# The loads of the attention weights move from SP's queue to GpSimd's

## The chip, the cores and the metric

The kernel runs on one core of one Trainium2 chip. The metric is the device time of one execution in microseconds (us). Before the change the median of 3 runs is 724.13 us (721.79 to 724.44). A core has these engines: PE (TensorE, matmuls; its weight loads are shown as PEld), DVE (VectorE), ACT (ScalarE), POOL (GpSimd) and SP (SyncE), and 16 DMA engines that move data between DRAM and the on-chip memory. Each engine runs its own instructions in order and waits on semaphores for the others.

## The reference, cut to what matters

The reference is one transformer layer: cross attention of 8 batches of 112 tokens (width 512) to 375 context rows (width 256) with 16 heads of 128, and then a feed-forward part whose weights and activations are rounded to whole numbers of 8 bits. All of it is float32 outside the rounding.

```python
q = rmsnorm((layernorm(x) @ Wq).reshape(B, Sq, H, D), gq)       # Wq: 512 x 2048
k = rmsnorm((ctx @ Wk).reshape(B, Skv, H, D), gk)               # Wk: 256 x 2048
v = (ctx @ Wv).reshape(B, Skv, H, D)                            # Wv: 256 x 2048
attn = softmax(einsum('bqhd,bkhd->bhqk', q, k) / sqrt(D))
x = x + einsum('bhqk,bkhd->bqhd', attn, v).reshape(B, Sq, H * D) @ Wo   # Wo: 2048 x 512
x = x + ffn(layernorm(x))          # two matmuls, rows and weights rounded, gelu between
```

## The kernel before, in words

The attention runs over 4 pairs of batches and, in each pair, over 4 groups of 4 heads: 16 *groups* (G), each of which has two *units* (u = 2G and 2G + 1), one for each batch of the pair. The weights of a group are one slice each: wq (1024 KB), wk (512 KB), wv (512 KB) and wo (1024 KB). They don't stay on the chip between the pairs, so each group loads its own four: 16 loads each of wq, wv and wo, and 15 of wk by the same function, as the first slice of wk comes in two halves (`load_half`, L222).

In a unit, PE makes the keys (`keys`, L632, tile pkk) out of the context and wk. ACT copies them out of PSUM and squares them, DVE sums, scales and transposes them in blocks of 32 (tile kz). The whole transposition goes by DRAM: `key_send` (L689) writes kz to kd with four DMAs, `key_fetch` (L696) reads it back as kT. The queries (`queries`, L514, tile pq, of wq) go by qz, qd (L569) and qr (L601) in the same manner, and ACT makes qT of qr (L608). PE makes the scores out of kT and qT (`scores`, L740, tile sc), DVE and ACT the probabilities, and these go by pz, pd (`prob_send`, L789) and pT (`prob_fetch`, L799). PE weighs the context with pT (`weigh`, L842, tile pu), and both units of a group together go through wv (`values`, L869, tile po) and wo (`project`, L889, tile pw; for the last group `project_rows`, L912). The tokens (xd, xr, xnT) and the context rows (cd, cr) have their own ways by DRAM. The feed-forward part of the batches that are done (ph L1079, py L1158) is woven in between; its weights are loaded in pieces at the start (`load_piece`, L307), and `max_weight` finds their largest magnitude with an all-reduce over partitions on GpSimd (L322), twice in all.

What runs when is written out by hand: four scripts of words (L1214 to L1364, played by `play`), in which `lq`, `lk`, `lv`, `lo` are the four loads and a number after the dot is the group. `in_written_order` (L77) then chains the instructions of PE, DVE, ACT and SP so that each keeps the order of the script:

```python
ORDERED = (ENG.PE, ENG.DVE, ENG.Activation, ENG.SP)
```

GpSimd isn't in this list (L26). On it, the framework's scheduler decides the order, from the instructions' dependencies.

All loads and all transfers by DRAM are issued by SP, in the script's order. So a weight load goes out when SP comes to it and its buffer is free. The buffers: wk has two, wq, wv and wo one each. The load of group 1's wq takes wo's buffer, that of the last wo takes wq's, and that of the last wv takes one of wk's. A load waits until the last matmul that reads the tenant before is done. The framework also gives each DMA that SP issues one of eight completion semaphores in turn, and many an issue waits until the DMA that had this semaphore before has landed.

Of the kernel before, what the change touches and what calls it, by code (L numbers as in the profile page):

```python
# [30 lines left out]
def xattn_ffn_kernel(  # L31
# [16 lines left out]
    nc = tc.nc  # L48
    P = 128
# [7 lines left out]
    NG = INNER // (HG * D)  # L57
    GW = HG * D
# [65 lines left out]
    n = 1  # L124
# [84 lines left out]

    def load_wq(G):  # L210
        t = wpool.tile([P, KC, GW], F32, tag="wo" if G == 1 else "wq", name=f"wq_{G}")
        nc.sync.dma_start(out=t, in_=wq[:, bass.ts(G % NG, GW)].rearrange("(k p) n -> p k n", p=P))
        T["wq", G] = t

    def load_wk(G):
        t = T["wk", G] = wpool.tile([P, KCC, GW], F32, tag="wk", name=f"wk_{G}", bufs=2)
        if G > 0:
            nc.sync.dma_start(out=t, in_=wk[:, bass.ts(G % NG, GW)].rearrange("(k p) n -> p k n", p=P))

    def load_half(k):  # L220

# [3 lines left out]
    def load_wv(G):  # L225
        tag, bufs = ("wk", 2) if G == NGG - 1 else ("wv", 1)
        t = wpool.tile([P, KCC, GW], F32, tag=tag, name=f"wv_{G}", bufs=bufs)
        nc.sync.dma_start(out=t, in_=wv[:, bass.ts(G % NG, GW)].rearrange("(k p) n -> p k n", p=P))
        T["wv", G] = t

    def load_wo(G):
        t = wpool.tile([P, HG, C], F32, tag="wq" if G == NGG - 1 else "wo", name=f"wo_{G}")
        nc.sync.dma_start(out=t, in_=wo[bass.ts(G % NG, GW), :].rearrange("(h p) c -> p h c", p=P))
        T["wo", G] = t

    def pad_context(b):
# [26 lines left out]
    def load_biases(_):  # L263
        after(("jr", 2 * NP - 1))
        nc.sync.dma_start(out=b1_sb, in_=b1.partition_broadcast(P))
        nc.sync.dma_start(out=b2_sb, in_=b2.partition_broadcast(P))

    step("lq", NG, load_wq)
    step("lk", NG, load_wk)
    step("lv", NG, load_wv)  # L270
    step("lo", NG, load_wo)
    step("cz", BP, pad_context)
    step("lc", BP, load_context)
# [1127 lines left out]
```

## Time and profile before

| | us |
|---|---|
| median of 3 runs | 724.13 |
| lowest, highest | 721.79, 724.44 |
| the profiled execution | 723.51 |
| its span, from the first instruction to the last | 721.4 |
| granted TensorE clock in it (mean) | 0.999 |

In the profile's rows, a line such as "pq<-wq,xnT" tells the tile that is written and those that are read, "L514" the line of the kernel, and a row of waits has the total, the number and the longest. The DMA part gives for each transfer the number of issues, the size and the median time from issue to landing:

| transfer | issues | KB each | median us to landing |
|---|---|---|---|
| kd<-kz (keys out) | 128 | 192 | 4.8 |
| kT<-kd (keys back) | 32 | 768 | 5.8 |
| pT<-pd (probabilities back) | 31 | 672 | 6.0 |
| qr<-qd (queries back) | 26 | 224 | 5.7 |
| wq<-in_wq | 16 | 1024 | 8.1 |
| wo<-in_wo | 16 | 1024 | 7.9 |
| wv<-in_wv | 16 | 512 | 5.9 |
| wk<-in_wk | 15 | 512 | 6.0 |

These 63 loads of the four weights are 15 x 0.5 + 16 x 0.5 + 32 x 1 = 47.5 MiB, or 49.8 of the 191.85 MB that the one queue moves. A DMA's "landing" is the time at which its last completion count arrives.

### The profile page before, as it was taken

The page shows a single profiled execution, that of the slowest core. Times are in us where ns is not written, and L with a number is a line of the kernel's source. Part 1 is how long each engine was busy: PE and PEld are TensorE (multiplying, and loading weights), DVE is VectorE, ACT ScalarE, POOL GpSimd, SP SyncE. Part 2 cuts the span into 40 slices and gives each one's busy share as a digit, 9 for nine tenths or more (in the row PEclk, how much of TensorE's full clock was granted, in tenths as well). Part 3 has the DMA queues.
Part 4 walks back from the last instruction along what each step waited for, and adds up shares of the span by engine and source line. Part 5 has one row for each costly group of instructions (what it writes and reads, how often), then busy time and mean ns, then how long its engine had stood idle before and what let it go on. Part 6 is the DMA issues. An engine that isn't in the chain of part 4 may idle for free.

```text
span 721.4 us, 8447 instructions
## 1 busy us (share of the span) xinstructions
PE 701.9 (97%) x2324; PEld 404.1 (56%) x2324; DVE 541.6 (75%) x1249; ACT 437.7 (61%) x1128; POOL 2.7 (0%) x10
## 2 busy tenths in 40 slices
PE   7999999999999999999999999999999999999986
PEld 3444474746557474655556566555665546576642
DVE  6897988768778798668655878687864788874686
ACT  3677757646485764666727564784755477545555
POOL 0000000000000000000000000000000000000000
PEclk9999999999999999999999999999999999999999
DMA  8899999989998999998999889999899998997300
GB/s 265 266 332 313 283 310 357 270 284 331 316 319 279 296 275 277 304 267 273 294 294 294 281 244 285 290 258 296 252 226 308 295 250 263 246 273 267 89 15 29
DMA packets 134125, 192.36 MB, mean 267 GB/s; under 512 B 35184, under 2 KB 93168, under 8 KB 133440
## 3 DMA queue, kind: packets, MB, share of 16 engines
q1 hardware_dynamic: 134080, 191.85, 86.6%
q8 instruction: 18, 0.29, 0.2%
q14 instruction: 27, 0.22, 0.1%
HBM read 126.81 MB, written 61.71 MB: 261 GB/s over the span
## 4 chain that ended last, share of the span: by engine, by line
PE 70%; DMA 17%; DVE 5%; ACT 4%; SPq 2%; issue 1%; DVEq 0%; ACTq 0%
PE pkk L632 17%; PE pu L842 15%; PE pq L514 10%; PE pw L889 9%; PE sc L740 8%; PE po L869 6%; DMA qr<-qd 3%; PE ph L1079 2%; DMA pT<-pd 2%; DMA wq<-in_wq 2%; DMA cT<-in_ctxT 2%; DMA kT<-kd 2%; DMA kd<-kz 1%; DMA wo<-in_wo 1%; DMA qss<-s 1%
## 5 line engine op out<-in xcount | busy, mean ns | idle before, releaser
L632 PE MATMUL pkk<-wk,cT 128*128 128x512 f32 x372 | 170.2, 592 | 0.1
L842 PE MATMUL pu<-pT,c 128*128 128x448 f32 (+1 forms) x384 | 152.0, 540 | 1.9 <-DMA pT<-pd 1.6
L762 ACT ACTIVATE probs<-sc,bias,rq 112x375 f32<-112x375 f32 x128 | 84.4, 664 | 50.5 <-DVE bias L755 48.6
L842 PEld LDWEIGHTS pu<-pT,c 128*128 128x128 f32 (+1 forms) x384 | 72.3, 190 | 74.1 <-issue 62.2
L632 PEld LDWEIGHTS pkk<-wk,cT 128*128 128x128 f32 x372 | 70.2, 190 | 73.9 <-issue 63.6
L514 PE MATMUL pq<-wq,xnT 128*128 128x512 f32 x224 | 101.1, 594 | 3.9 <-DMA wq<-in_wq 2.7
L889 PEld LDWEIGHTS pw<-oT,wo 128*128 128x128 f32 x480 | 90.8, 190 | 8.4 <-issue 4.4
L740 PE MATMUL sc<-kT,qT 128*112 128x384 f32 x256 | 93.9, 487 | 1.4 <-DMA kT<-kd 0.9
L889 PE MATMUL pw<-oT,wo 128*128 128x224 f32 x480 | 94.6, 352 | 0.0
L652 ACT COPY kk<-pkk 128x512 f32<-128x512 f32 x96 | 55.4, 580 | 61.9 <-PE pkk L632 25.0
L663 DVE TENSOR_REDUCE kss<-ksq 128x4 f32<-128x512 f32 x96 | 63.4, 669 | 32.9 <-ACT ksq L657 32.2
L779 DVE STREAM_TRANSPOSE pz<-probs 128x384 f32<-128x384 f32 x124 | 66.1, 556 | 14.8 <-ACT probs L773 13.6
L773 ACT ACTIVATE probs<-probs,inv 112x375 f32<-112x375 f32 x128 | 72.6, 600 | 5.5 <-DVE inv L770 3.8
L753 DVE TENSOR_REDUCE top<-sc 112x1 f32<-112x375 f32 x128 | 63.8, 536 | 15.8 <-PE sc L740 15.5
L514 PEld LDWEIGHTS pq<-wq,xnT 128*128 128x128 f32 x224 | 42.1, 190 | 55.8 <-issue 48.0
L680 DVE STREAM_TRANSPOSE kz<-kk 128x512 f32<-128x512 f32 x96 | 64.9, 693 | 8.6 <-DMA kd<-kz 6.8
L740 PEld LDWEIGHTS sc<-kT,qT 128*112 128x112 f32 x256 | 44.7, 177 | 42.6 <-issue 19.0
L657 ACT ACTIVATE ksq<-kk 128x512 f32<-128x512 f32 x96 | 59.6, 628 | 8.0 <-DVE kss L663 7.5
L670 DVE TENSOR_TENSOR kk<-kk,rk 128x512 f32<-128x512 f32 x96 | 62.9, 676 | 0.3
L853 ACT COPY wc<-pu 128x448 f32<-128x448 f32 x64 | 33.2, 528 | 38.0 <-PE pu L842 38.0
L869 PEld LDWEIGHTS po<-wc,wv 128*128 128x128 f32 x272 | 49.1, 190 | 7.4 <-issue 3.1
L869 PE MATMUL po<-wc,wv 128*128 128x224 f32 (+1 forms) x272 | 52.9, 344 | 0.0
(122 smaller groups left out, 597.7 us busy)
## 6 DMA issues: line engine op xcount, KB each, us to landing
kd<-kz SPq DMA_DIRECT2D x128, 192.0 KB, 4.8
kT<-kd SPq DMA_DIRECT2D x32, 768.0 KB, 5.8
pT<-pd SPq DMA_DIRECT2D x31, 672.0 KB, 6.0
pd<-pz SPq DMA_DIRECT2D x93, 192.0 KB, 3.8
wq<-in_wq SPq DMA_DIRECT2D x16, 1024.0 KB, 8.1
wo<-in_wo SPq DMA_DIRECT2D x16, 1024.0 KB, 7.9
wv<-in_wv SPq DMA_DIRECT2D x16, 512.0 KB, 5.9
wk<-in_wk SPq DMA_DIRECT2D x15, 512.0 KB, 6.0
```

The costliest lines, as they stand in the source:

```text
L514: nc.tensor.matmul(pq[:, :GW], T["xnT", p][:, k, i * P : (i + 1) * P], T["wq", G][:, k, :], start=(k == 0), stop=(k == KC - 1),)
L632: nc.tensor.matmul(pk[:, :GW], T["cT", batch_of(u)][:, k, j * P : (j + 1) * P], T["wk", u // BP][:, k, :], start=(k == 0), stop=(k == KCC ...
L663: nc.vector.tensor_reduce(T["kss", u][:, j, :], T.pop(("ksq", u, j)).rearrange("p (h d) -> p h d", d=D), AX.X, ALU.add)
L680: nc.vector.transpose(T["kz", u][:, :, j, :, :].rearrange("p a h r -> p h a r"), T["kk", u][:, j, :].rearrange("p (h a r) -> p h a r", h=H ...
L740: nc.tensor.matmul(sc[:S, :SKP].rearrange("p (j i r) -> p j i r", j=NJ, r=BK), T["qT", G, i][:, h, :], T["kT", u][:, :, :, h, :].rearrange ...
L753: nc.vector.tensor_reduce(top[:, h : h + 1], T["sc", u, h0 + h][:S, :SK], AX.X, ALU.max, negate=True)
L762: nc.scalar.activation(p_bufs[h][:S, :SK], T["sc", u, h][:S, :SK], AF.Exp, bias=T["bias", u, h0][:, h - h0 : h - h0 + 1], scale=rq_of(u, h ...
L773: nc.scalar.mul(p_bufs[h][:S, :SK], p_bufs[h][:S, :SK], T["inv", u][:, h : h + 1])
L779: nc.vector.transpose(T["pz", u][:, :, :, :, h, :].rearrange("p a f j q -> p j a f q"), p_bufs[h].rearrange("p (j a r) -> p j a r", j=NJ, ...
L842: nc.tensor.matmul(pu[:, : HG * S], T["c", b][: ROWS[j], j, k * P : (k + 1) * P], T["pT", u][: ROWS[j], :, j, :, :].rearrange("p f h q -> ...
L869: nc.tensor.matmul(po[:, (h - h0) * n : (h - h0 + 1) * n], T["wv", G][:, k, h * D : (h + 1) * D], T["wc", G][:, k, h, :, :].rearrange("p b ...
L889: nc.tensor.matmul(pw[:, (c - c0) * n : (c - c0 + 1) * n], T["wo", G][:, h, c * P : (c + 1) * P], T["oT", G][:, h, lo : lo + n], start=(h ...
```

## The change

The four functions that load a group's weights issue their DMA on GpSimd (`nc.gpsimd`) instead of SP (`nc.sync`). Source, destination, size and the place of the call in the script are the same. `load_half`, the loads of x, context, gains, biases and feed-forward weights, and all transfers by DRAM stay on SP.

```diff
     def load_wq(G):
         t = wpool.tile([P, KC, GW], F32, tag="wo" if G == 1 else "wq", name=f"wq_{G}")
-        nc.sync.dma_start(out=t, in_=wq[:, bass.ts(G % NG, GW)].rearrange("(k p) n -> p k n", p=P))
+        nc.gpsimd.dma_start(out=t, in_=wq[:, bass.ts(G % NG, GW)].rearrange("(k p) n -> p k n", p=P))
         T["wq", G] = t
...
         if G > 0:
-            nc.sync.dma_start(out=t, in_=wk[:, bass.ts(G % NG, GW)].rearrange("(k p) n -> p k n", p=P))
+            nc.gpsimd.dma_start(out=t, in_=wk[:, bass.ts(G % NG, GW)].rearrange("(k p) n -> p k n", p=P))
...
-        nc.sync.dma_start(out=t, in_=wv[:, bass.ts(G % NG, GW)].rearrange("(k p) n -> p k n", p=P))
+        nc.gpsimd.dma_start(out=t, in_=wv[:, bass.ts(G % NG, GW)].rearrange("(k p) n -> p k n", p=P))
...
-        nc.sync.dma_start(out=t, in_=wo[bass.ts(G % NG, GW), :].rearrange("(h p) c -> p h c", p=P))
+        nc.gpsimd.dma_start(out=t, in_=wo[bass.ts(G % NG, GW), :].rearrange("(h p) c -> p h c", p=P))
```

## The prediction, made before the changed kernel was run

> **What bounds the kernel now.** I read the shares of the engines first, then the DMA queues, the stretches, the waits of PE and of SP, and last the timeline around single loads. The first part of the page and the row of its 40 slices for DMA:
>
> ```profile
> PE 701.9 (97%) x2324; PEld 404.1 (56%) x2324; DVE 541.6 (75%) x1249; ACT 437.7 (61%) x1128; POOL 2.7 (0%) x10
> DMA  8899999989998999998999889999899998997300
> q1 hardware_dynamic: 134080, 191.85, 86.6%
> ```
>
> PE is idle for 721.4 - 701.9 = 19.5 us, GpSimd nearly always. All bytes go by one queue. The stretches (us, then busy time of PE, PEld, DVE, ACT, POOL, granted clock, DMA share, GB/s) tell where PE's idle time is:
>
> ```profile
> 0.00:20.00 20.00, 16.33 (x32) 7.12 (x33) 12.11 (x50) 7.48 (x18) 1.67 (x8) 1.00 0.82 261
> 20.00:100.00 80.00, 80.00 (x225) 40.24 (x224) 70.36 (x160) 58.02 (x177) 0.71 (x1) 1.00 0.93 300
> 100.00:200.00 100.00, 98.12 (x311) 57.83 (x310) 80.25 (x171) 59.83 (x158) 0.00 (x0) 1.00 0.94 314
> 300.00:400.00 100.00, 97.22 (x323) 57.97 (x322) 64.86 (x144) 58.11 (x151) 0.00 (x0) 1.00 0.94 284
> 660.00:721.00 61.00, 52.75 (x258) 30.75 (x257) 40.53 (x92) 32.54 (x55) 0.00 (x0) 0.99 0.23 66
> ```
>
> 3.7 us lie before 20, 8.3 after 660, where no weight is loaded; only 7.5 us lie between. DMA is at 0.93 to 0.94 of its time there: the second resource that is nearly full, whose order of work can cost PE time. PE's waits that a DMA ended, and three of SP's on a weight:
>
> ```profile
> PE pq L514 <- DMA wq<-in_wq: 2.7, 2, 1.4
> ...
> PE pu L842 <- DMA pT<-pd: 1.6, 3, 1.1
> ...
> PE pq L514 <- DMA xnT<-xld: 1.2, 2, 0.7
> PE sc L740 <- DMA kT<-kd: 0.9, 2, 0.6
> ```
>
> ```profile
> SPq L689 <- DMA wq<-in_wq: 5.4, 3, 2.8
> SPq L689 <- DMA wo<-in_wo: 4.6, 2, 2.5
> SPq L569 <- DMA wq<-in_wq: 3.4, 2, 2.5
> ```
>
> So weights delay PE by 2.7 us in all, and they hold up SP's sends of keys (L689) and queries (L569). SP's waits that end at a weight's landing add up to 31.0 us over all eleven such groups, but most are hidden: the whole of PE's DMA waits in these four rows is 6.4 us.
>
> **The change, part by part.** PE, DVE and ACT keep their instructions and order. SP loses 63 DMAs (15 wk, 16 each of wq, wv, wo); GpSimd gains them. The order on GpSimd isn't that of the script: the built program has it by the time at which each load's buffer comes free. I set each load's free time (end of the last matmul on the buffer's tenant before) against its need (first matmul on the new one) from the matmuls' times in the trace. Before, SP issues most loads 10 to 45 us after their buffer is free (wq of group 4: free 98.1, issued 138.9, needed 151.0). On GpSimd nothing holds them. The two maxima (L322), which stand in the same queue, ran at 96.1 and 204.1; the loads behind them come free at 98.1 and 218.6, so they cost nothing; were the first as late as 131, the wo load of group 1 (needed 135.0) would be late.
>
> (a) *Lateness.* The smallest rooms from free to need are wq 6: 13.2 us, wo 14: 13.6, wq 9: 13.9, wo 13: 16.0, wo 10: 17.9, wq 3: 18.2. A wq took 5.0 / 8.1 / 12.8 us (min, median, max) from issue to landing, a wo 6.4 / 7.9 / 11.7. Even at the maximum they land in time. PE's two waits on wq (at 190.0 and 358.1) go, as these loads leave 21.7 and 4.7 us earlier: -2.7.
>
> (b) *The start.* Four loads (wk 1, wq 0, wv 0, wq 1: 512 + 1024 + 512 + 1024 KB) have no predecessor in their buffers. GpSimd's memsets end at 2.2, so all 3 MB can be queued some 3 us into the span; before, they left at 5.7, 6.5, 21.1 and 30.3. They meet the loads that PE waits for:
>
> ```profile
> 1.65 4.82 DMA cT<-in_ctxT
> 6.47 0.14 issue
> 6.60 8.42 PE pkk L642 x12
> ```
>
> This stretch of the chain is start, length, what. x landed at 3.40; the next wk and cT halves, 443.5 KB, took the 3.07 us until 6.47. Sharing the engines half and half from there would double that: +3.1 at most, 0 if GpSimd's first bytes come after 6.5. The rest has a little spare (the x pair lands at 9.7 and DVE waits 2.75 us for it, then has 1.9 us idle at 12.5). I take +2.0, nearer the upper end because GpSimd is free so early.
>
> (c) *Issue time and SP's waits.* A load's issue took SP about 0.43 us, 63 x 0.43 = 27 us in all, and the 31.0 us above go too. On the path this is worth between 0 and the 3.7 us that PE waits for pT, xnT and kT. I take -1.2, a third: most of these fetches wait for their own stores (SP's rows on kd and pd are 14.7 and 14.2 us).
>
> The Trainium skill, "DMA: Bandwidth & Descriptors", section on issuing engines not being separate DMA queues, says that all issuers share the same 16 DMA engines and that a second issuer only saves issue time. Going by it alone, (c) would be the whole gain and (a) no more than a matter of order; the rows on PE's wq waits say that order is worth 2.7.
>
> (d) *Collisions.* Loads that leave 20 us earlier run beside other transfers than before. For every fetch with under 2 us from landing to first use I compared the time that loads are in flight from its store to its landing, before and with the new issue times (a landing as before, stretched to half rate). Most meet less, but these, with next to no spare, meet more: qr landing at 110.6 (4.8 to 14.3 us), kT at 277.3 (8.9 to 13.2), kT at 325.3 (0 to 9.8: wo 6 and wk 10 now leave at 312.1 and 313.8), pT at 328.5 (0 to 4.4).
>
> ```profile
> 321.16 0.34 SPq L696 DMA_DIRECT2D kT<-kd  x1
> 323.32 0.34 SPq L799 DMA_DIRECT2D pT<-pd  x1
> ...
> 325.48 2.81 PE L740 MATMUL sc<-kT,qT 128*112 128x384 f32 x8 [0.26 <-DMA kT<-kd]
> ```
>
> That kT landed 4.1 us after its issue with no weight beside it; the median is 5.8 and the maximum 9.3. So a collision costs 5.8 - 4.1 = 1.7, at most 5.2. Three at 1.7 less 0.1 of spare, and 0.8 for pT (5.2 there against a median of 6.0): 1.6 x 3 + 0.8 = 5.6; bounds 0 and 4 x 5.2 = 20.8. PE then stops in order, and score, exponential and sends behind it move along. I take +5.0, since a stall gives spare to the next.
>
> (e) *Making the transfers on GpSimd.* No row has a DMA issued by GpSimd. Its time to issue is bounded below by SP's 0.43 us and above, as an estimate, by the 5.0 us that remain of the smallest room after a median landing (13.2 - 8.1): past this, loads come late. Beside it, DVE could be held up. DVE's 2048-wide TENSOR_SCALAR takes 1287 ns where the 2048-wide TENSOR_REDUCE takes 2272: it runs nearly twice as fast for an element, on some 55 us of such work in all. If each of 63 loads held DVE for as long as GpSimd's all-reduce took (mean 532 ns), that were 33 us of DVE time, a quarter of it (DVE's idle share is 25%) perhaps on the path: 0 to +8. I take +1.0, because only 8% of the span is such work.
>
> The skill speaks against the change here: "SBUF — State Buffer", section "SBUF: two separate sides", says that a GpSimd-issued DMA has its descriptors written by GpSimd's cores, which a two-port VectorE operation locks out until it ends. By it the 1287 ns above are the longest delay of a load, under every room in (a), so the sum by it has 0 for (e).
>
> **Sum.** -2.7 + 2.0 - 1.2 + 5.0 + 1.0 = +4.1 us. The profiled execution took 723.51 us with its span of 721.4; 723.51 + 4.1 = 727.6. The median of the runs shown, 724.13, is 0.6 above that execution, so I forecast 728.2, 0.6% over it.
>
> **Rivals.** *Weights out of SP's way* (faster): small transfers no longer queue behind 1 MB, so every wait of PE on a DMA goes and nothing is lost at the start or to collisions: 724.13 - 6.4 = 717.7. For it: most tight fetches meet less load, and SP's 31.0 us. Against: DMA stays at 0.94 full. It decides if the median landing of kT falls below about 4.8 us, one under today's.
>
> *Nothing moves* (same): the start's loss takes up the gain at the waits (+2.0 - 2.7 + 0.5 of (c) and (d) together), 724. For it: PE's idle time between 20 and 660 is but 7.5 us, and most loads have over 20 us of room. Against: tight fetches at 0.0 to 0.1 us.
>
> *Late loads* (much slower): if a 1 MB load takes 20 us from GpSimd's issue, the six rooms above are short by 6.8, 6.4, 6.1, 4.0, 2.1 and 1.8: +27, some 751; at 16 us it is +7.3 by the first three (2.8, 2.4, 2.1), which on top of the forecast without the gain of (a) is 728.2 + 2.7 + 7.3 = 738. For it: no row prices a GpSimd DMA. Against: rooms half as large again as the median landing.
>
> That the change doesn't do what it says: the order isn't the same, as shown; that is within the sum.
>
> **How the numbers follow.** Chances: the forecast 0.38 (its own range 727.8 to 735), late loads 0.12, same 0.25, weights out of the way 0.25. Runs of this kernel differ by about 0.4% (721.79 to 724.44), so 0.5% is about what a measurement tells from none: slower 0.50, same 0.25, faster 0.25. The range for 8 in 10 leaves out a little of the faster case below 717 and most of the late loads above 738; it holds (b) and (c) at both ends and (d) up to half its upper bound.
>
> **What would show it.** A second queue in the DMA part with 49.8 MB. (a) No row PE L514 <- DMA wq; loads issued at their buffers' free times. (b) The first pkk L642 later than 6.60, by 0 to 3.1. (c) SP's waits on w loads gone. (d) More of PE's waits on kT, pT and of ACT on qr, at about 110, 277 and 320 to 330; kT's median landing above 5.8. (e) Waits of DVE that end at POOL, and GpSimd's own time. I am wrong if PE's idle time between 20 and 660 falls under 5 us, or if any matmul waits for a weight.

## The result and the profile after

| | before | after |
|---|---|---|
| median, us | 723.57 (720.74 to 724.44, 6 runs) | 763.92 (759.92 to 772.54, 6 runs) |
| ratio, 95% interval | 1 | 1.0563 (1.0523 to 1.0603) |
| span of the profiled execution, us | 721.4 | 761.7 |
| PE busy / idle in it, us | 701.9 / 19.5 | 713.9 / 47.8 |

The change makes the kernel 5.6% slower. The forecast was 728.2 us with a range to 738: the direction is right, the size is wrong by 36 us. Here and below the medians are of all executions, and a ratio, with its 95% interval, is to the kernel before in the same rounds without the executions that are over 1.5% above the fastest of their kernel (one of the six after).

The first part of the page after, with its rows for the granted clock, the DMA engines and the queues:

```profile
PE 713.9 (94%) x2324; PEld 407.6 (54%) x2324; DVE 541.3 (71%) x1249; ACT 437.5 (57%) x1128; POOL 50.9 (7%) x73
PEclk9899999999999999999999999999999999989999
DMA  9689989799997988978987988978898968986210
q1 hardware_dynamic: 108752, 142.03, 61.5%
q0 software_dynamic: 13168, 49.81, 20.2%
```

The weights are now on a second queue (49.81 MB). DVE's and ACT's busy times are unchanged. PE is idle for 28.3 us more, and its same 2324 matmuls take 12.0 us longer: 40.3 us in all, the whole growth of the span.

The stretches (us, busy time of PE, PEld, DVE, ACT, POOL, granted clock, DMA share, GB/s) show both:

```profile
20.00:100.00 80.00, 73.64 (x187) 33.38 (x186) 64.20 (x150) 53.18 (x162) 4.41 (x6) 0.96 0.85 268
300.00:400.00 100.00, 96.78 (x302) 54.71 (x301) 67.61 (x158) 56.68 (x151) 6.63 (x9) 0.97 0.86 266
```

Before, PE was busy for all 80 us from 20 to 100, at a clock of 1.00, with DMA at 0.93. Now it is idle for 6.4 us of them, the clock is 0.96 and DMA is *less* busy, 0.85. So over the stretch as a whole bandwidth hasn't run out: transfers come in an order that lets PE run dry.

The 12.0 us come from the clock. It is granted at 0.50 in six stretches of 3.4 or 6.8 us (from 20, 170, 300, 351, 504 and 672 us), each in or behind a wait of PE of 1.9 to 5.9 us, and at 1.00 elsewhere until 760. PE works for 23.5 us in these six, and half of that is 11.7. Not each wait has such a stretch: there is none behind the 3.0 us at 87 and the 2.8 us at 615. One of the six, and the wait at 87:

```profile
170.00:173.00 3.00, 3.00 (x5) 1.21 (x4) 2.39 (x6) 2.13 (x5) 0.00 (x0) 0.50 0.21 70
87.00:95.00 8.00, 4.68 (x13) 2.16 (x14) 5.89 (x13) 4.47 (x12) 0.00 (x0) 1.00 0.88 275
```

PE's waits (total, count, longest):

```profile
PE sc L740 <- DMA kT<-kd: 6.3, 5, 2.5
PE py L1158 <- DVE hid L1088: 5.9, 1, 5.9
PE pu L842 <- ACT kk L652: 3.9, 2, 2.8
...
PE pu L842 <- DMA pT<-pd: 2.7, 3, 1.8
```

No row has a weight. The two waits on wq are gone, and waits on round trips through DRAM have come: kT, pT, and steps of ACT and DVE that are late because a transfer ahead of them was. Followed back, those at 78, 121, 415, 475 and 585 us of before come to a q of 5.70 us, a qr of 14.16, an s of 7.31, a kd of 6.18 and an rt of 5.88 (medians before: 3.8, 5.7, 5.8, 4.8, 4.5). The one on hid is of this kind too. Its chain (start, length, what):

```profile
661.44 11.71 DMA qss<-s
...
673.49 0.65 DVE hid L1088
...
674.18 1.87 PE py L1158 x4
```

DVE works in order and stands until 673.15 for a query's statistics, whose way by DRAM took 11.71 us (median 3.8 before); hid comes behind them, and PE waits for hid.

I also set each matmul's start beside its start in before. The delay grows by 7.3 us until 18.7 us, then by steps of 1 to 6 us at about ten places (78 to 83, 121, 152, 277, 325, 414, 476, 547, 585 and 635 us of before), shrinks by 1.1 to 2.3 at five places, two of them the former waits on wq (1.5 at 190, 1.6 at 358), and ends at 40.3.

### The profile page after: what moved, and what is told of

Its sections match the earlier page's. It is cut to its first block, busy times and chain, and to the rows that moved or that the text cites. A ratio compares the mean times of both kernels' runs of the same rounds, so it can differ in the third digit from the quotient of the medians.

```text
span 761.7 us, 8518 instructions
## 1 busy us (share of the span) xinstructions
PE 713.9 (94%) x2324; PEld 407.6 (54%) x2324; DVE 541.3 (71%) x1249; ACT 437.5 (57%) x1128; POOL 50.9 (7%) x73
## 3 DMA queue, kind: packets, MB, share of 16 engines
q0 software_dynamic: 13168, 49.81, 20.2%
## 4 chain that ended last, share of the span: by engine, by line
PE 39%; DMA 29%; DVE 14%; SPq 8%; ACT 7%; issue 2%; DVEq 0%; ACTq 0%
PE pu L842 10%; PE pkk L632 6%; DMA kd<-kz 6%; PE pw L889 5%; PE sc L740 5%; PE pq L514 5%; PE po L869 3%; DMA pd<-pz 3%; DMA q<-qz 3%; DMA kT<-kd 3%; DMA pT<-pd 3%; DVE kz L680 3%; SPq L689 2%; DMA gk_sb<-in_gk 2%; PE py L1158 2%
## 5 line engine op out<-in xcount | busy, mean ns | idle before, releaser
L632 PE MATMUL pkk<-wk,cT 128*128 128x512 f32 x372 | 174.4, 603 | 6.5 <-ACT kk L652 3.1
L632 PEld LDWEIGHTS pkk<-wk,cT 128*128 128x128 f32 x372 | 70.9, 192 | 83.1 <-issue 67.2
L514 PE MATMUL pq<-wq,xnT 128*128 128x512 f32 x224 | 104.0, 608 | 2.2 <-DMA xnT<-xld 2.2
L740 PE MATMUL sc<-kT,qT 128*112 128x384 f32 x256 | 96.0, 497 | 6.8 <-DMA kT<-kd 6.3
```

The source lines that it names most:

```text
L514: nc.tensor.matmul(pq[:, :GW], T["xnT", p][:, k, i * P : (i + 1) * P], T["wq", G][:, k, :], start=(k == 0), stop=(k == KC - 1),)
L632: nc.tensor.matmul(pk[:, :GW], T["cT", batch_of(u)][:, k, j * P : (j + 1) * P], T["wk", u // BP][:, k, :], start=(k == 0), stop=(k == KCC ...
L740: nc.tensor.matmul(sc[:S, :SKP].rearrange("p (j i r) -> p j i r", j=NJ, r=BK), T["qT", G, i][:, h, :], T["kT", u][:, :, :, h, :].rearrange ...
```

## The experiments

Two suspects stand behind the steps. *Time*: loads leave up to 45 us before their place in the script. *Queue*: on GpSimd's queue a load no longer stands in line with SP's transfers. And the start is a case by itself. The first four kernels separate the three.

**Only the start, and all but the start.** The four loads are wk 1, wq 0, wv 0, wq 1.

```diff
+    def queue_of(kind, G):
+        return nc.gpsimd.dma_start if (kind, G) not in START else nc.sync.dma_start
```

For the start alone the condition is the other way round.

> The changed kernel with the four loads that the start needs (wk 1, wq 0, wv 0, wq 1) back on SP at their places; the other 59 stay on GpSimd. The curve of PE's delay puts 7.3 us at the start by 18.7 us. Theory START (the burst of 3 MB at the start is the whole of it): 724 us. Theories EARLY (loads issued up to 45 us before their place take engines from SP's small transfers) and QUEUE (a second queue takes its turn packet by packet, whenever its loads are issued): both 763.9 - 7.3 = about 756.6, range 752 to 760, and the first matmul of L642 back near 6.6 us.

> The kernel before with only those four loads on GpSimd, 59 on SP. START: 764 us. EARLY and QUEUE: 723.6 + 7.3 = about 731, range 728 to 734; the later delays (277, 325, 635 us) are absent.

Measured: the start alone 731.42 us, ratio 1.0083 (1.0042 to 1.0123), as expected. All but the start 763.04, ratio 1.0516 (1.0436 to 1.0596): no gain can be told from the changed kernel's 763.9, where 7.3 us were expected. In its profile the delay at the start is absent, but by 84 us it is 10.5 us all the same. A likely reason, which no run tests: a stall at one place gives spare to the chains behind it, so the parts don't add up. START as the whole cause falls.

**The same queue at the script's times.** Each of the 59 loads on GpSimd gets a semaphore wait on ScalarE's last instruction written ahead of its word:

```diff
+            prev = [i for i in block.instructions if i.engine == ENG.Activation][-1]
+            ins = nc.gpsimd.dma_start(out=out, in_=in_).ins
+            tc.add_manual_dep(ins, prev.name, edge, reason="held to the script's place")
```

> As with the start back on SP, and each of the 59 loads on GpSimd waits for the last ScalarE instruction written ahead of its place in the script, which in the trace of before ends 2 us after to 9.5 us before SP issued that load (median 1.3 us before). So the queue is GpSimd's and the time is that of before. EARLY: 722 to 730 us, near before. QUEUE: 745 to 757 us, most of what is left of the loss stays. The waits of PE at kT, pT and hqT are gone by EARLY, and still there by QUEUE.

**The early times on SP's queue.** Fifty-five words are moved up in the four scripts, as here:

```diff
-kq1.3 z2.0 qf0.1 z3.0 k2.4 kc1.4
+kq1.3 z2.0 qf0.1 lo.0 z3.0 k2.4 kc1.4
...
-jl.1 s0.3 kt1.4 lo.0 kr2.5 kc0.6 ks.4
+jl.1 s0.3 kt1.4 kr2.5 kc0.6 ks.4
```

> The counterpart: all loads on SP, but 55 of the words for them are moved up in the script to just behind the first transfer that SP issued after the buffer was free in the trace of before, so that they are issued within some microseconds of when GpSimd would; the start is that of before. EARLY: 745 to 757 us. QUEUE: 720 to 730 us (the two waits on wq, 3 us together, may go).

Measured: held on GpSimd 745.65 us, ratio 1.0276 (1.0214 to 1.0338); early on SP 755.84, ratio 1.042 (1.0352 to 1.0488). Each lies where the theory put it that makes that suspect the cause: so both are, and neither theory holds alone. The early times cost more *without* GpSimd than GpSimd costs without them. In the early version on SP, PE's largest wait is on kT:

```profile
PE sc L740 <- DMA kT<-kd: 12.9, 5, 5.4
```

**How exact must "the script's times" be?** The held version was off by -9 to +2.5 us. So: GpSimd held closer, and SP with the held version's errors put in.

```diff
+        for word in AFTER.split():
+            kind, G, name, at, engine, n = word.split(",")
+            ins = [i for i in SEEN[name, int(at)] if str(i.engine).endswith(engine)][int(n)]
+            tc.add_manual_dep(HELD[kind, int(G)], ins.name, edge, reason="held to SP's time of before")
```

AFTER names for each load the ScalarE or VectorE instruction. In the version on SP the words are moved as above, by smaller steps.

> 59 loads on GpSimd again (the start's four on SP), each now held to the ScalarE or VectorE instruction whose end in the trace of before was closest to 0.8 us ahead of SP's issue of that load (0.4 us is what GpSimd took from such an end to its issue, 0.4 us what its loads landed later): within -1.3 and +1.0 us of the times of before, where the first held version was off by -9 to +2.5 us and took 745.7 us. PLACE (what costs is that a load falls in front of or beside an urgent small transfer that the script had kept clear of it; the queue is nothing): 722 to 730 us. QUEUE (the second queue itself takes from the small transfers): 740 to 748 us, as the first held version.

> All loads on SP, but the words of 32 of them are moved in the script by what the first held version was off by (-8 to +3 us, mostly 2 to 5 us early), to the nearest gap between SP's transfers. PLACE: the loss of the first held version comes back without GpSimd, 738 to 750 us. QUEUE: 722 to 728 us.

Measured: close hold 740.27 us, ratio 1.0172 (1.012 to 1.0223); SP with the errors 732.96, ratio 1.01 (1.0054 to 1.0147). Both numbers lie between the theories' ranges or at their edge. Together (ratios):

| loads issued | by SP | by GpSimd |
|---|---|---|
| at the times of before | 1 | 1.0172 |
| off by some 2 to 8 us | 1.0100 | 1.0276 |
| as soon as the buffer is free | 1.0420 | 1.0516 |

A few microseconds' shift costs 1% on either queue. What the queue does shows in the close hold where PE waits longest. (The profiled execution took 747.42 us against the median of 740.27, so its waits are longer than usual.) PE's largest row, and the chain that ended last (start, length, what):

```profile
PE pu L879 <- DMA pT<-pd: 18.1, 5, 6.2
```

```profile
551.25 6.18 DMA pd<-pz
...
557.58 8.72 DMA pT<-pd
...
566.43 1.83 PE pu L879 x2
```

Before, the last of the four pieces of P (the probabilities, sent as pd) landed 3.6 us after its issue (537.43 to 540.99), SP issued pT at 541.11 and only *then* wk 15, wo 11 and wq 14 (542.02, 542.45, 543.61); pT landed in 5.8 us. Before on SP, then the close hold on GpSimd:

```profile
541.11 0.34 SPq L799 DMA_DIRECT2D pT<-pd  x1
541.54 0.38 SPq L582 DMA_DIRECT2D s<-qss  x1
542.02 0.38 SPq L218 DMA_DIRECT2D wk<-in_wk  x1
```

```profile
551.07 0.70 POOL L236 DMA_DIRECT2D wv<-in_wv  x1 [23.79 <-PE pkk L669]
554.04 0.72 POOL L236 DMA_DIRECT2D wk<-in_wk  x1 [2.27 <-ACT probs L799]
```

In the close hold GpSimd issues wv 11 at 551.07, beside the last piece of P, and the other three loads at 554.04 to 555.60, while SP still waits for P. They are all ahead of pT, whose issue is late, and PE waits 6.2 us. On SP a late P held up the loads behind it; on GpSimd nothing does, and the order of SP's script binds only what is on SP. "DMA: Bandwidth & Descriptors" of the Trainium skill, section "Queues, rings and completion order", says that an engine alternates between queues packet by packet. The 6.18 and 8.72 us agree with that but don't single it out.

One rival has no run. On SP the loads take turns with the small transfers in eight completion semaphores, and SP's waits at a weight's landing are 36.2 us before; on GpSimd the loads have eight semaphores of their own, and after the change SP has no such wait. So the move also lets more transfers be under way at a time, and no version holds that fixed while it changes the queue.

**Does a lost order explain it?** Each load on GpSimd waits until the transfer ahead of it on SP has landed (the edit against the first held version):

```diff
-            prev = [i for i in block.instructions if i.engine == ENG.Activation][-1]
+            prev = [i for i in block.instructions if i.engine == ENG.SP][-1]
```

> 59 loads on GpSimd (the start's four on SP), each held until the transfer that SP issued ahead of its place has landed, some 3 to 9 us later than SP issued it in before; so no load can run beside a small transfer that stood ahead of it in the script, though it can beside those behind it. ORDER (GpSimd costs because a load there overtakes the urgent transfers that stood ahead of it on SP, where a late P or k held it back): the waits of PE for kT and pT shrink to those of before (6 to 8 us in all), and what is added are late weights, which had 0.1 to 30 us to spare in before; 724 to 738 us, below the 740.3 of the close hold. SHARE (the second queue takes its turn beside small transfers, whichever come first): 740 us or more, with waits for kT and pT as long as there.

Measured 768.39 us, ratio 1.0649 (1.058 to 1.0718). The time misses both. The waits on small transfers went as ORDER has it, kT and pT together 4.7 us where the close hold has 20.5 and before 2.5. That alone proves little, since a PE that stands for weights also gives these fetches time. And the weights are late:

```profile
PE pq L527 <- DMA wq<-in_wq: 13.5, 2, 7.7
PE pw L902 <- DMA wo<-in_wo: 12.3, 4, 8.1
```

There is no room to hold the loads back either. The next pair splits the 59 loads of the close hold by whether a kT or pT issued ahead of them on SP was still under way in before (30) or not (29). The edit is against the close hold.

```diff
-        if (kind, G) in START:
+        if (kind, G) in ON_SP:
```

> The close hold, but the 30 loads that SP issued in before while a transfer of kT or pT that it had issued ahead of them was still on its way go back to SP; 29 stay on GpSimd, and 7.3 fewer MB by a second queue beside kT and pT. ORDER: nearly all of the loss of the close hold (740.3 against 725.9) is these 30, so 724 to 730 us, and no wait of PE for pT over 2 us. SHARE (any load on the second queue costs alike): half of the loss, 731 to 735 us.

> The counterpart: only those 30 loads on GpSimd with the close hold, the other 29 on SP. ORDER: 735 to 742 us, with waits of PE for pT of 3 to 6 us as in the close hold. SHARE: 731 to 735 us.

Measured: the 30 back on SP 728.97 us, ratio 1.0034 (0.9999 to 1.007); the 30 alone on GpSimd 730.44, ratio 1.0043 (1.0018 to 1.0069). The first is in ORDER's range, the second below both. PE's waits on pT are where ORDER put them, here with the 30 back on SP, then with them on GpSimd:

```profile
PE pu L887 <- DMA pT<-pd: 1.9, 3, 1.0
```

```profile
PE pu L887 <- DMA pT<-pd: 7.1, 3, 3.4
```

The second profile has idle times of 2.0, 1.0, 3.4 and 2.8 us ahead of the same four units of pu as the close hold has 3.4, 4.3, 6.2 and 2.9 (at 83, 374, 547 and 670 us of before); the first has none over 1.1 there. But the times don't follow: both halves cost 0.3 to 0.4%, less than half of 1.7% each. In these profiles ORDER fits at the four places, not in the total, and not in every execution: the version with halved loads below holds all 59 on GpSimd to the same instructions, and its profile, of an execution of 731.31 us, has 1.1 us at the first of the four units and nothing at the others. Why the halves don't add up to the whole stays open.

**Is it the earliness or the neighbours?** On SP alone: 39 loads up to 48 us early, but into gaps; and 31 loads hardly moved, but to just ahead of a transfer of k or P.

```diff
-kr2.4 kc0.5 ks.3 kr1.4 s2.2 iv.1
+kr2.4 kc0.5 ks.3 lk.4 kr1.4 s2.2 iv.1
...
-a1.0 s2.4 sb.3 lk.4 kr1.6 s3.4 ks.5
+a1.0 s2.4 sb.3 kr1.6 s3.4 ks.5
```

That is one of the 39; in the other version the same word goes between qf0.3 and S1.3, ahead of sb.3.

> All loads on SP. 39 of the 59 are moved up by 4 to 48 us (20 us on average), as early as their buffer was free, but only to places where by the trace of before SP issues no transfer of k or P (kd, kT, pd, pT) for the next 3 us (512 KB) or 4 us (1 MB); the other 20 stay. The first early version on SP, which took the first place after the buffer was free whatever followed, took 755.8 us. EARLY (the earliness itself costs): 740 to 755 us. PLACE (what costs is what is issued right behind the load): 722 to 732 us.

> All loads on SP. 31 of the 59 are moved by at most 8 us (23 earlier, 8 later) to the nearest place directly ahead of SP's issue of a kT, a pT or a pd. PLACE: 738 to 755 us, with waits of PE for kT and pT of 10 us and more in all. EARLY: 722 to 730 us, since the loads are on average 1.5 us earlier than in before.

Measured: early into gaps 754.34 us, ratio 1.0382 (1.0298 to 1.0467), in EARLY's range; in front 752.16, ratio 1.0369 (1.0287 to 1.0452), in PLACE's, with 15.8 us of waits on pT, again ahead of the same four units (2.2, 6.3, 4.9 and 2.0 us). So each theory has one run. The chain of the first one tells why "gaps" failed, at its longest wait:

```profile
424.59 0.54 SPq L218
...
427.89 7.13 DMA q<-qz
...
441.90 5.05 DMA qd<-qz
...
447.43 5.91 DMA kT<-kd
```

SP issued a wo and a wk at 424.11 and 424.59, in a gap of k and P; the wk landed at 433.99. Behind them stood a query's qd and q, which landed at 434.21 to 435.01: q took 7.13 us (median 3.8 in before). DVE's work on it came late, the next qd stood behind one more load (a wq, issued at 437.55, landed at 446.06; qd 446.25 to 446.96), and with them the issue of kT came late, and PE waited 5.6 us. The median landing of kT in this run is 5.9 us, as in before (5.8). The loads didn't slow the transfer that PE waits for; they slowed ones several steps ahead of it. My set of urgent transfers was too small. A chain of the one longest wait is shown; that all 29 us arise so isn't.

**The price of one place.** Three words moved by 1 to 3 us, all on SP:

```diff
-kt2.2 pf.-1 s7.1 kt1.2 w0.-2 lk.3 x1.0 kc0.4 lo.-1 kq0.4 qf0.1 lq.2
+kt2.2 lk.3 lo.-1 lq.2 pf.-1 s7.1 kt1.2 w0.-2 x1.0 kc0.4 kq0.4 qf0.1
```

> The kernel before with three words moved by 1 to 3 us: wk 15, wo 11 and wq 14 (2.6 MB) stand directly ahead of the pT that SP issued at 541.1 us, instead of one to four transfers behind it. In before that pT landed at 546.9 and PE used it at 547.5, with 0.5 us to spare. PLACE: 2.6 MB at the 265 GB/s of before are 9.8 us that pT lands later, so PE waits some 9 us, and 2 us more for the clock after the wait: 733 to 737 us. If transfers of one queue do not hold each other up, or the place has slack that the trace hides: 724 to 726 us.

> Only these three loads on GpSimd, within 1.3 us of their times of before, the other 60 on SP at their places. ORDER or SHARE at this one place: they run beside that pT instead of behind it; pT landed 8.7 us after its issue in the close hold, against 5.8, and PE waited 3.4 us for it in the run with 30 loads on GpSimd: 727 to 731 us. If the cost of GpSimd is spread and not at single places: 724.5 to 726 us.

Measured: three ahead on SP 730.01 us, ratio 1.0072 (1.0045 to 1.01), some 5 us for three words; expected were 8 to 12 or none. The same three on GpSimd 726.42, ratio 1.0011 (0.9987 to 1.0035): no cost that can be told, and under the range of ORDER and SHARE. (In its profile, of an execution of 733.74 us, pT took 8.8 us and PE waited 3.6 us for it; the median doesn't bear that out.) The chain, and the stretch behind the wait, of the version on SP:

```profile
544.82 4.30 DMA pd<-pz
...
549.26 11.29 DMA pT<-pd
...
560.68 1.83 PE pu L842 x2
```

```profile
560.60:566.00 5.40, 5.32 (x10) 2.65 (x11) 0.00 (x0) 1.29 (x3) 0.00 (x0) 0.71 1.01 313
```

pT took 11.29 us where it had taken 5.83. PE waited 5.9 us for it. In the next 5.4 us the granted clock was 0.71, with PE busy throughout: 1.6 us more by the matmuls' starts. The place adds 7.6 us in all, and later waits gave back 2.3: 5.3, as the medians say. The profiled execution took 736.98 us, more than the median, because PE was already 7.2 us late ahead of the place, where no word had been moved; 3.5 of them are one wait for a kT at 81 us of before. So a wait of some 3 us at one place of a single profile can be chance.

**Three more.** The loads issued by ScalarE, for another queue with hardware descriptors (the edit against the version with the start back):

```diff
-        return nc.gpsimd.dma_start if (kind, G) not in START else nc.sync.dma_start
+        return nc.scalar.dma_start if (kind, G) not in START else nc.sync.dma_start
```

> The 59 loads issued by ScalarE, in its order, at the script's places (the start's four on SP): times within -9 to +2.5 us of before, as in the first held version, but with hardware descriptors. PLACE: 738 to 752 us, as there, plus ScalarE's issue time where it is on the path. QUEUE, if it is the software queue's 4096-byte packets that matter: 724 to 732 us, and packets of 2048 bytes.

Measured 817.18 us, ratio 1.1245 (1.1197 to 1.1293), with 2048-byte packets (22784 of them). It says nothing on packets, since other waits came in. The loads here take turns with SP's DMAs in the same eight completion semaphores. In the chain of the longest wait SP issues pT only when ScalarE's wo, which had pT's semaphore before it, has landed:

```profile
419.05 8.71 DMA wo<-in_wo
...
427.81 7.00 DMA pT<-pd
```

Packets by GpSimd, halved:

```diff
+            h = out.shape[-1] // 2
+            HELD[kind, G] = [nc.gpsimd.dma_start(out=out[:, :, n * h : (n + 1) * h], in_=in_[:, :, n * h : (n + 1) * h]).ins for n in range(2)]
```

> The close hold with each of the 59 loads cut into two of half the columns, so that a row's run is 1024 bytes instead of 2048; the same bytes at the same times, GpSimd's issue time doubled (0.7 us more a load). PACKET (each queue gets its turn by packet, so 4096-byte packets push aside the 256- to 1536-byte ones of SP's small transfers): packets shrink and the loss with them, 728 to 736 us. If packets or their size do not matter: 738 to 745 us.

Measured 742.04 us (731.31 to 746.73), ratio 1.0164 (1.0079 to 1.025). The trace still has 11392 packets of 4096 bytes, as the close hold: the edit didn't change what it was to change, so the packet theory is untested.

And an attempt to beat the kernel before, from the one part of the change that did what was forecast. Two words move on SP; shown is that of wq 9 (lq.5 of the second script).

```diff
-ka.10 bo.-1 e2.7 ps.6 xc.4 iv.7
+ka.10 bo.-1 e2.7 lq.5 ps.6 xc.4 iv.7
...
-p1.2 S1.4 ke.10 lq.5 sb.4 kc0.11 ks.9
+p1.2 S1.4 ke.10 sb.4 kc0.11 ks.9
```

> The kernel before with two words moved on SP: wq 5 by 5.1 us earlier, wq 9 ahead of the four transfers of P of unit 14 (2 to 3 us earlier). In before PE waits 1.5 and 1.3 us for these two. If these are the only weights that were late: 721 us, ratio 0.996. If the load of wq 5 or of wq 9 collides in its new place: 725 to 730.

Measured 727.04 us against 725.9 beside it, ratio 0.9991 (0.9959 to 1.0023). In its profile PE's row on wq shrinks from 2.7 to 0.5 us, but kT's is 5.0 where it was 0.9. No version here beats the kernel before.

## Why the prediction was wrong, by its steps

- **(a) Lateness, -2.7: right.** No matmul waits for a weight, and the delay shrinks by 1.5 and 1.6 us at the two places named. Got on SP alone, by moving two words, it made no difference that could be told; in that profile the waits on kT are longer instead.
- **(b) The start, +2.0 (0 to 3.1): right sign, too small.** Measured 7.3 us by 18.7 us in the profile after and 0.8% (6 us) alone. The bound of 3.1 came from the wk and cT halves until 6.47 and those do agree (first pkk L642 at 7.60 instead of 6.60). The rest is behind: cT 1 landed at 18.39 instead of 10.59, the x pair at 14.80 instead of 9.70, and the gains at 19.92 instead of 10.97, which DVE waits for in order:

```profile
5.06 14.86 DMA gk_sb<-in_gk
...
19.95 0.16 DVE gqk L261
```

- **(c) SP's issue time, -1.2: no such gain seen.** SP's waits on weights went (36.2 us in nineteen rows; the 31.0 of the prediction are the eleven largest), but kT's median landing is 5.7 us (5.8 before) and pT's 6.3 (6.0). The sign that I gave for collisions, a median of kT above 5.8, didn't come either: medians don't show this loss, the longest do (pT's maximum went from 9.1 to 13.4 us).
- **(d) Collisions, +5.0: the step that failed.** That loads beside the small transfers make PE wait is right, and three of the four named places cost. At 277 and 325 PE's waits for kT grow by 2.2 us each, and with the slower clock behind them the delay by 3.9 and 3.8, against the 1.7 each that I gave them. The qr of 110.6 took 14.16 us instead of 8.83, and reached PE by a way that I hadn't looked at: the last of SP's next four sends of keys waited for its landing, then DVE for that send, and PE lost 1.9 us at 121.

```profile
112.37 14.16 DMA qr<-qd
...
126.55 6.43 DMA kd<-kz
...
133.06 0.71 DVE kz L680
```

The pT of 328 cost nothing. But the term of (d) had to be some 33 us: the delay grows by 33 us between 18.7 us and the end. Three things were wrong in (d). It took only fetches that land within 2 us of use, and not the legs ahead of them: of the 28.3 us of idle time that PE gains, only 6.5 are in its rows on kT and pT, and in the run into gaps too the delay begins several steps ahead. It took the price of a collision from landing times (1.7 us), while three loads ahead of one pT cost PE 5.9 us. And it left out the clock: of the 40.3 us, 12.0 are the same matmuls at a lower clock around PE's idle times. It was also worked out on the times of before; after the first stall the loads and SP's chains no longer stand to each other as in that list.
- **(e) Making the transfers, +1.0 (0 to 8): about nothing.** DVE's busy time is 541.3 us (541.6). GpSimd takes 0.71 to 0.83 us (means of the four weights) to issue a load, against SP's 0.43; PE waits for no load. The lock that the Trainium skill tells of there, "SBUF — State Buffer", section "SBUF: two separate sides", shows in none of PE's waits.
- **The rivals.** Weights out of SP's way needed a kT under 4.8 us: 5.7. Nothing moves fell with the start alone. Late loads had a time near the measured one (751) by a mechanism that didn't occur. The order isn't the same was named and waved off as within the sum; the early order alone, on SP, costs 4.2% of the 5.6%. The forecast took order as a matter of each load's own deadline, and not of what each load stands in front of.

Two slips of the prediction don't change its sum: a weight is still loaded after 660 us (the last wo, 664.81 to 671.27), and 13.2 - 8.1 is 5.1.

The Trainium skill's rule that I set beside (c), "DMA: Bandwidth & Descriptors", section "Issuing engines are not separate DMA queues", by which a second issuer saves only issue time, differs from the measurement: even at about the times of before the second issuer cost 1.7% (1.2 to 2.2%), and 1.6% (0.8 to 2.5%) with the loads halved.

What stays open: how the 33 us divide between early times and the second queue (1.042 and 1.0172 alone, 1.0516 together), whether the second queue costs by the lost order, by sharing the engines or by its own eight semaphores, why halves of the close hold cost so little, and whether packet size matters.

## What to carry to other kernels

A hand-placed queue order can be worth more than the loads' deadlines show: before moving a bulk load, ask which small transfers stand right behind it, and follow each of their chains up to the matmul, not only the last fetch. Issuing from a free engine also gives up what the in-order queue did unasked, which is to hold bulk loads back when an urgent transfer is late. In this kernel a stall of PE cost its idle time and, on average, a quarter to two fifths more by the slower clock around it (1.6 us after 5.9; 12.0 beside 28.3). And a wait in one profile should be seen in a second one, or in the times, before a cause is read from it.

## What the runs showed of the hardware that was not expected

- Around PE's idle times the granted clock falls to 0.50 for 3.4 or 6.8 us: six times in the profile after, with waits of 1.9 to 5.9 us, while waits of 2.8 and 3.0 us had no such stretch behind them. Mean time of a 128x512 matmul of L632 went from 592 to 603 ns over the whole kernel.
- The loads of the weights went as 2048-byte packets from SP and ScalarE and as 4096-byte packets from GpSimd, and halving the rows' runs to 1024 bytes left GpSimd's packets at 4096.
- DMA engines at 0.85 with PE waiting for transfers: from 20 to 100 us two queues moved 268 GB/s, one had moved 300.
- A gain vector of 128 elements took 14.86 us to land beside the 3 MB of the start, 5.9 before; the 375 KB of context issued 1.5 us ahead of it took 14.84.
